# The order in which a selective scan's input is loaded: two rounds of six channels

## The chip, the cores and the metric

The kernel runs on one core of one Trainium2 chip. The metric is the device time of one execution in microseconds (us); the kernel before was run three times, and its median counts.

## What is computed

The reference is a network of four layers over four images of 64 x 64 pixels with 96 channels. Layers 0 and 1 are of one kind, and nearly all of the time lies in them. Each normalises its input, projects it to 192 channels, applies a 3 x 3 convolution and a SiLU, and then runs a selective scan along the 4096 pixels in four directions (by rows, by columns, and both backwards). Cut to what matters:

```python
delta = softplus(dts @ dt_w + bias)             # for image, direction k, channel e, pixel l
def step(h, inp):                               # 16 states n for every channel
    u, d, b, c = inp
    h = exp(d[..., None] * A) * h + d[..., None] * b[:, :, None, :] * u[..., None]
    y = einsum('bken,bkn->bke', h, c)
    return h, y
out = scan(step, h0, (u, delta, B, C)) + u * D
```

The four directions are added, normalised, gated by SiLU(z), projected back and added to the input. Layers 2 and 3 (linear attention and a quantised feed-forward block) follow, and the change does not touch them.

## The kernel before

**Stages.** `Scans.run` (L701) goes over four phases: two layers times two pairs of images. For each it runs `prepare` (normalisation, projection, convolution, delta and so on, interleaved with `finish` of the phase before) and then `scan_phase` (L471). At the end `token_layers` does layers 2 and 3.

**What `prepare` leaves in DRAM.** `steps` (L285) writes delta as three bf16 parts, B and C (`ph.bc`), and the product delta * u as float32 (`ph.du`, L160). The product is written twice: `ph.du` is laid out [2 copies, G = 8 rows, 192 channels + 2, 512 pixels], where a row is one image in one direction.

**The scan stage.** A unit is a chunk of 512 pixels and a block of 12 channels (EB), for all 8 rows and 16 states at once: 128 partitions are 8 rows times 16 states. There are 8 chunks x 16 blocks = 128 units in a phase. For one unit:

- `load` (L386) takes a buffer `h` of 128 partitions x 12 channels x 512 pixels (four buffers), loads delta by `load_delta` (L374, the tile `dlt`, 72 partitions) and delta * u by six calls of `load_quarters` (L396). Every row of `du` is broadcast to four partitions of a quarter. A quarter is 32 partitions; partitions 32 to 95 are filled by one DMA that reads both copies (768 KB), the upper quarter (96 to 127) by one that reads copy 1, the lower one (0 to 31) by one that reads copy 0 (384 KB each). All of these carry six channels (n = EB // 2), so there are two DMAs for each of the three groups of partitions.
- `times_b` (L408, the multiplication at L411) multiplies h by B on POOL, three channels at a time: four instructions a unit. It runs six channels (B_LEAD) ahead of the scans.
- `replicate` and `decay` (L413, L419) make exp(delta * A): a matmul of PE spreads delta over the partitions, and ACT takes the exponential.
- `scan` (L425, the instruction at L428) is one scan along the pixels on DVE for each channel: twelve a unit.
- `contract` (L437) multiplies by C and sums over the states on PE one unit later, `evict` copies the sum to SBUF, and `store` (L462) writes it with four DMAs to `ph.y`.

**What sets the order.** The scan stage lies within a manual schedule: every engine works through its instructions in the order in which the program issues them, written out by hand in L508 to L544. At the end of unit `at` SP's queue gets, in this order: the four stores of unit `at - 1`, sometimes a load of B or C, and the loads of unit `at + 3` (delta first, then the six of h). The buffer of unit `at + 3` is that of unit `at - 1`, whose contraction ends in unit `at`. Every DMA that SP issues signals one of eight semaphores in turn, and waits first for the DMA that used this semaphore before, eight DMAs earlier. A POOL product waits for the loads that wrote its three channels: the products of channels 0 to 5 for the three DMAs of the first six channels, the others for the other three.

The part of `load` that matters:

```python
n = EB // 2
for first, quarters in ((1, 2), (3, 1), (0, 1)):
    for e in range(0, EB, n):
        self.load_quarters(u, e, n, first, quarters)
```

`first` is the first quarter that is written and `quarters` how many: (1, 2) is partitions 32 to 95, (3, 1) the upper quarter, (0, 1) the lower one.

Of the kernel before, what the change touches and what calls it, by code (L numbers as in the profile page):

```python
# [32 lines left out]
EB = 12  # L33
# [49 lines left out]
class Consts:  # L83
# [3 lines left out]
    def load(self, pool, name, shape):  # L87
        t = pool.tile(shape, F32, name=name)
        self.nc.sync.dma_start(t, self.a[name])
        return t  # L90
# [40 lines left out]
class Scans:  # L131
# [19 lines left out]
    def prepare(self, ph):  # L151
# [16 lines left out]
        with self.tc.tile_pool(name="prep", bufs=1) as wp, self.tc.tile_pool(  # L168
# [3 lines left out]
            def load(name, shape, at=0):  # L172
                t = wp.tile([at + shape[0]] + shape[1:], F32, name=name)
                nc.sync.dma_start(t[at:], a[pre + name])
                return t

            xp = load("x_proj", [C, 2, 2, XD2])
            dt_w = load("dt_w", [XD2 - 2 * NS, 2, E], at=2 * NS)
            conv_b = load("conv_b", [C, 2])
            ds = load("Ds", [C, 2, K])  # L180
            dsum = wp.tile([C, 2], F32, name="dsum")
# [204 lines left out]
    def load(self, u):  # L386

        nc, ph = self.nc, u.ph
        u.h = self.units.tile([128, EB, TC], F32, name="h", bufs=4)
        self.load_delta(u)  # L390
        n = EB // 2
        for first, quarters in ((1, 2), (3, 1), (0, 1)):
            for e in range(0, EB, n):
                self.load_quarters(u, e, n, first, quarters)

    def load_quarters(self, u, e, n, first, quarters):  # L396
# [594 lines left out]
```

## Time and profile before

| | |
|---|---|
| median of three runs | 12278.37 us (12270.65 to 12295.46) |
| the profiled execution | 12285.39 us, of which the span 12283.6 us |
| the four scan stages | 743 to 2650, 3556 to 5458, 6366 to 8270 and 9176 to 11079 us of the span |
| busy in the first of them (1907 us) | DVE 1805 us, POOL 1755 us, PE 1444 us, ACT 1287 us; DMA engines 0.74 on average, 249 GB/s |
| loads of h (L401) | 1024 DMAs of 768 KB and 2048 of 384 KB |

The scan stages take 7616 us of the 12283.6 us. A profile describes one execution, and its durations come from this one alone. A row of the page's group table gives the line, the engine, the operation, what is written and read, the number of instructions, then their busy time and the mean of one in ns, and last the engine's idle time ahead of them with what ended most of it. In the waits a row gives who waited for whom, the sum in us, how often, and the longest wait. "DMA share" is the mean busy share of the core's 16 DMA engines. The chain of waits follows the work that ended last back to the start of the span.

### The profile page before, as it was taken

The page shows a single profiled execution, that of the slowest core. Times are in us where ns is not written, and L with a number is a line of the kernel's source. Part 1 is how long each engine was busy: PE and PEld are TensorE (multiplying, and loading weights), DVE is VectorE, ACT ScalarE, POOL GpSimd, SP SyncE. Part 2 cuts the span into 40 slices and gives each one's busy share as a digit, 9 for nine tenths or more (in the row PEclk, how much of TensorE's full clock was granted, in tenths as well). Part 3 has the DMA queues.
Part 4 walks back from the last instruction along what each step waited for, and adds up shares of the span by engine and source line. Part 5 has one row for each costly group of instructions (what it writes and reads, how often), then busy time and mean ns, then how long its engine had stood idle before and what let it go on. Part 6 is the DMA issues. An engine that isn't in the chain of part 4 may idle for free.

```text
span 12283.6 us, 340681 instructions
## 1 busy us (share of the span) xinstructions
PE 9393.5 (76%) x147008; PEld 4897.8 (40%) x147008; DVE 9369.7 (76%) x9235; ACT 7066.9 (58%) x11815; POOL 7389.7 (60%) x2316
## 2 busy tenths in 40 slices
PE   7757777769877777769877777778877777777777
PEld 2224444433334444433334444443334444444333
DVE  2479999963569999982569999993459999993667
ACT  2456666643456666653456666662446666662556
POOL 0159999950149999970129999980119999990000
PEclk8669898889778988889778988888778888988787
DMA  3577777754667777764667777764567777773110
GB/s 94 170 226 256 251 252 252 251 166 140 205 206 253 251 252 255 252 201 123 183 206 253 252 251 254 251 226 125 173 194 250 253 253 252 252 252 124 19 21 11
DMA packets 906195, 2491.48 MB, mean 203 GB/s; under 512 B 278030, under 2 KB 560756, under 8 KB 773236
## 3 DMA queue, kind: packets, MB, share of 16 engines
q1 hardware_dynamic: 578036, 2163.43, 52.6%
q10 hardware_dynamic: 326656, 306.25, 8.5%
q8 instruction: 1158, 18.97, 0.7%
q14 instruction: 345, 2.83, 0.1%
HBM read 1955.47 MB, written 513.80 MB: 201 GB/s over the span
## 4 chain that ended last, share of the span: by engine, by line
DMA 57%; PE 20%; SPq 9%; DVE 5%; ACT 4%; issue 3%; POOL 1%; ACTq 1%; DVEq 0%; POOLq 0%
DMA h<-du 51%; SPq L401 8%; PE c L263 8%; PE f L596 2%; PE d L309 2%; DMA yk<-y 2%; DMA delta<-parts 1%; PE c L292 1%; PE f L687 1%; PE f L605 1%; DMA du<-du_sb 1%; POOL parts L323 1%; PE f L676 1%; DVE parts L324 1%; PE f L662 1%
## 5 line engine op out<-in xcount | busy, mean ns | idle before, releaser
L411 POOL TENSOR_TENSOR h<-h,b 128x1536 f32<-128x1536 f32 x2048 | 7019.3, 3461 | 603.8 <-DMA h<-du 230.7
L428 DVE TENSOR_TENSOR_SCAN h<-a,carry,h 128x512 f32<-128x512 f32 x5376 | 6346.6, 1259 | 238.3 <-POOL h L411 231.9
L421 ACT ACTIVATE a<-a,a_col 128x512 f32<-128x512 f32 x6144 | 4030.4, 664 | 1917.7 <-PE a L417 1885.8
L446 PEld LDWEIGHTS y<-h,cw 128*32 128x32 f32 x131072 | 2789.8, 129 | 3520.4 <-issue 1302.1
L446 PE MATMUL y<-h,cw 128*32 128x48 f32 x131072 | 3663.3, 266 | 537.8 <-DVE h L428 210.6
L417 PE MATMUL a<-dlt,rep 72*128 72x512 bf16 x6144 | 2562.4, 428 | 1339.9 <-DVE h L428 1242.8
L323 POOL CAST parts<-dl 96x1024 bf16<-96x1024 f32 x256 | 342.1, 1351 | 3108.6 <-DVE dl L320 2742.6
L319 DVE TENSOR_TENSOR du_sb<-dl,xc 96x1024 f32<-96x1024 f32 x256 | 397.0, 1577 | 1294.6 <-ACT dl L317 1242.0
L458 ACT COPY d<-y 128x384 f32<-128x384 f32 x2048 | 979.7, 478 | 490.5 <-PE y L446 449.4
L263 PE MATMUL c<-xn,taps 96*96 96x512 f32 x2304 | 1036.8, 611 | 73.7 <-DVE xn L248 52.8
L428 DVE TENSOR_TENSOR_SCAN h<-a,h 128x512 f32<-128x512 f32 x768 | 873.0, 1203 | 176.9 <-ACT a L421 139.2
L417 PEld LDWEIGHTS <-rep 72*128 72x128 bf16 x6144 | 490.8, 99 | 888.7 <-issue 646.5
L309 PE MATMUL d<-xd,dt_w 7*96 7x512 f32 x1024 | 523.0, 859 | 260.0 <-ACT xd L295 227.4
L263 PEld LDWEIGHTS c<-xn,taps 96*96 96x96 f32 x2304 | 383.6, 168 | 709.9 <-issue 631.2
L828 POOL MEMSET tn<- 1x4096 f32 x8 | 28.0, 3533 | 863.2 <-PE pa L848 514.2
L270 ACT ACTIVATE xc<-c,conv_b 96x512 f32<-96x512 f32 x128 | 87.3, 682 | 716.0 <-PE c L263 646.4
L596 PE MATMUL f<-yk,perm 128*128 128x384 f32 x1024 | 417.3, 547 | 96.6 <-DMA yk<-y 87.2
L324 DVE TENSOR_TENSOR parts<-dl,parts 96x1024 bf16<-96x1024 f32 x256 | 366.9, 1455 | 154.3 <-POOL parts L323 154.3
L317 ACT ACTIVATE dl<-d 96x1024 f32<-96x1024 f32 x256 | 252.0, 1017 | 402.3 <-DMA delta<-parts 230.6
L292 PE MATMUL c<-xc,x_proj 96*103 96x512 f32 x512 | 422.1, 961 | 2.5 <-ACT xc L270 2.5
L309 PEld LDWEIGHTS d<-xd,dt_w 7*96 7x96 f32 x1024 | 152.3, 212 | 548.3 <-ACT xd L295 299.0
L363 ACT ACTIVATE cw<-c,gmask 128x256 f32<-128x256 f32 x512 | 285.7, 569 | 119.2 <-DMA c<-bc 61.9
(114 smaller groups left out, 5656.7 us busy)
## 6 DMA issues: line engine op xcount, KB each, us to landing
h<-du SPq DMA_DIRECT2D x1024, 768.0 KB
h<-du SPq DMA_DIRECT2D x2048, 384.0 KB
delta<-parts ACTq DMA_DIRECT2D x512, 288.0 KB
dlt<-delta SPq DMA_DIRECT2D x512, 288.0 KB
du<-du_sb SPq DMA_DIRECT2D x256, 384.0 KB
du<-du_sb ACTq DMA_DIRECT2D x256, 384.0 KB
y<-d SPq DMA_DIRECT2D x2048, 48.0 KB
yk<-y SPq DMA_DIRECT2D x256, 384.0 KB
```

The source lines that it names most:

```text
L263: nc.tensor.matmul(rows(ps[:C]), taps[:, tap, h * C : (h + 1) * C], xn[:, ROWS * c + dy : ROWS * (c + 1) + dy, dx : dx + HW], start=tap == ...
L292: nc.tensor.matmul(rows(ps[:XD2]), xp[:, k, h], u[:, h], start=h == 0, stop=h == 1)
L309: nc.tensor.matmul(ps[:, m], dt_w[part, k, m * C : (m + 1) * C], xd[part], start=True, stop=True)
L324: nc.vector.tensor_tensor(parts[:, 2], delta, parts[:, 1], ALU.subtract)
L401: self.nc.sync.dma_start(u.h[32 * first : 32 * (first + quarters), e : e + n].rearrange("p e t -> p (e t)"), source.rearrange("a g e t -> ...
L411: self.nc.gpsimd.tensor_tensor(h, h, b, ALU.mult)
L417: self.nc.tensor.matmul(u.a[n], self.cst.rep[:, h], u.dl[:, e], start=True, stop=True)
L421: self.nc.scalar.activation(u.a[n], u.a[n], AF.Exp, scale=u.ph.a_col[:, at : at + 1])
L428: self.nc.vector.tensor_tensor_scan(u.h[:, n], u.a.pop(n), u.h[:, n], 0.0 if u.c == 0 else u.ph.carry[:, at : at + 1], ALU.mult, ALU.add,)
L446: self.nc.tensor.matmul(view(u.y[32 * j : 32 * j + 32], l2 * EB, (8 * EB, 4), (1, EB)), u.ph.cw[u.c][:, l1, 8 * j + l2], view(u.h, 64 * l1 ...
L458: self.nc.scalar.copy(u.d[:, :, :, l1], u.y[:, : 32 * EB].rearrange("p (t h x) -> p t h x", t=4, h=2))
L596: nc.tensor.matmul(ps[:, : 4 * C].rearrange("p (w v e) -> p w v e", w=4, v=nv), cst.perm[:, k], view(t, off, (sw if k < 2 else -sw, 4), (1 ...
```

## The change

The two loops of `load` change places, so that all partitions get channels 0 to 5 before any gets channels 6 to 11, and the lower quarter comes before the upper one:

```diff
         n = EB // 2
-        for first, quarters in ((1, 2), (3, 1), (0, 1)):
-            for e in range(0, EB, n):
+        for e in range(0, EB, n):
+            for first, quarters in ((1, 2), (0, 1), (3, 1)):
                 self.load_quarters(u, e, n, first, quarters)
```

The number of DMAs, their sizes, their sources and what they write stay the same. On PE, ACT, DVE and POOL the instructions and their order are the same in both kernels; on SP only these six DMAs of a unit stand in another order.

## Prediction

> **What bounds the kernel now.** I read the page's engine shares and its chain first, then the waits of SP's queue, then the rate of the scans, and last the DMA queues in short windows. Names: a unit's six loads of h are M0 and M1 (partitions 32 to 95, channels 0 to 5 and 6 to 11), U0 and U1 (96 to 127), L0 and L1 (0 to 31); r0 to r3 are POOL's four products (L411) of three channels each. The page, its chain and two costly groups:
>
> ```profile
> DMA 57%; PE 20%; SPq 9%; DVE 5%; ACT 4%; issue 3%; POOL 1%; ACTq 1%; DVEq 0%; POOLq 0%
> ...
> L411 POOL TENSOR_TENSOR h<-h,b 128x1536 f32<-128x1536 f32 x2048 | 7019.3, 3461 | 603.8 <-DMA h<-du 230.7
> L428 DVE TENSOR_TENSOR_SCAN h<-a,carry,h 128x512 f32<-128x512 f32 x5376 | 6346.6, 1259 | 238.3 <-POOL h L411 231.9
> ```
>
> DMA leads the chain, though DVE is over 90% busy in the scan stages. DVE's idle time comes from POOL, and POOL's from DMA. Next the scans of 1600 us of the first scan stage, and an unbroken run of them:
>
> ```profile
> 1000.00:2600.00 1600.00, 1539.77 (x1306) 0.89 0.74 252
> ```
>
> ```profile
> 2002.68 33.19 DVE L428 TENSOR_TENSOR_SCAN h<-a,carry,h 128x512 f32<-128x512 f32 x28 [1.39 <-POOL h L411]
> ```
>
> 1600 / 1306 x 12 gives 14.70 us for a unit; unbroken, DVE needs 33.19 / 28 x 12 = 14.22 us, and POOL's four products 13.7. So 0.48 us of a unit is lost, always ahead of r0, which needs M0, U0 and L0. What holds the loads back is seen in SP's own waits in that window:
>
> ```profile
> SPq L401 <- DMA h<-du: 488.9, 303, 3.6
> ...
> SPq L401 <- POOL h L411: 6.2, 13, 0.7
> SPq L401 <- PE a L417: 5.4, 6, 1.0
> ```
>
> Each DMA of SP waits for the landing of the one eight before it, and this, not a buffer (POOL, PE), is what SP waits for. M0 is issued a median of 9 us after the unit whose end allows it. The queue is always full: the scan stages are bound by DMA at 14.7 us a unit.
>
> **The DMA engines.** Three windows of the first loads; columns are window, its length, PE, PEld, DVE, ACT, POOL, clock, DMA share, GB/s:
>
> ```profile
> 748.20:749.40 1.20, 1.20 (x5) 0.37 (x3) 0.00 (x0) 0.00 (x0) 0.00 (x0) 0.50 0.97 410
> 753.50:756.50 3.00, 0.00 (x0) 0.00 (x0) 0.00 (x0) 0.00 (x0) 0.00 (x0) 0.50 0.98 205
> 759.00:760.40 1.40, 0.00 (x0) 0.00 (x0) 0.00 (x0) 0.00 (x0) 0.00 (x0) 0.50 0.50 211
> ```
>
> From 759.0 only U1 or L loads run: half of the 16 engines, 211 GB/s. From 748.2 M0 and M1 run: all engines, 410 GB/s. From 753.5 all engines are busy too and move only 205 GB/s: by the order of issues, these are U packets of unit 0 on one half of the engines beside M0 and M1 of unit 1 on the other half. Their 12 KB packets last 930 to 950 ns instead of 460. The chain shows what that costs:
>
> ```profile
> 746.24 14.63 DMA h<-du
> 760.88 18.11 DMA h<-du
> 779.01 19.28 DMA h<-du
> 798.31 14.27 DMA h<-du
> ```
>
> The links of the next two loads are about 4 us longer than those around them.
>
> [...]In the trace the lower engines' order is that of the issues.
>
> So the lower eight engines carry all of U and L and half of M[...]; the upper eight carry M's other half[...]. [...]
>
> **The change, part by part.** It removes and adds no instruction: PE, ACT, DVE and POOL keep their order, and so do stores and delta loads. Bytes per engine are the same. Only the six loads of a unit change places: M0 M1 U0 U1 L0 L1 becomes M0 L0 U0 M1 L1 U1.
>
> *Base.* A lower engine moves four 12 KB packets of each load: 24 x 0.466 us (12,288 x 8 / 211 GB/s) = 11.2 us, plus 6 x 0.155 = 0.9 of delta and 0.5 of y: 12.6 us. Of the 14.7 us measured, 2.1 are contention. Following single engines' back-to-back packets, M0 takes some 2.4 us, M1 2.1, L1 2.3, U0 and L0 1.9.
>
> *Products released earlier.* r0 waits for the first three loads instead of the first, third and fifth, r2 for the last three. The last load still lands last. Behind a late r2 on POOL stand r3 and the next unit's r0; DVE's scan 6 waits for it. While DMA sets the pace this gains only at a stage's end, at most 14.2 - 7.1 - 1.9 = 5 us; the last three units of the first stage ran without a stall (36 scans on end), so I take 2.5 us x 4 = 10 us.
>
> *M1's upper half moves beside U0.* With M0's issue as zero, the median issues are 0, 2.65, 4.96, 5.69, 6.43 and 7.13 us, the first packet follows some 1.5 us later. The lower engines start M0 at 2.9, the second load at 5.6, the third at 8.0 (quartiles 1 us on either side). Now M1 is fourth: its upper half starts at 5.69 + 1.5 = 7.2 us. L0 (1.9 us, less than M1's 2.1) follows M0, so U0 runs from about 7.3 to 9.2: the same time. Both halve, as from 753.5. Fully aligned, an engine loses 4 x 0.466 = 1.86 us; with engines apart by about 1 us, I take 0.9 (bounds 0 and 1.86).
>
> *M0's upper half stands beside the U1 of the unit before.* [...]The upper half starts at 1.5 us; the lower engines end their sixth load at 0.9, 2.0 and 4.1 us (quartiles). What is left then is lost: 0, 0.5 and 1.86, about 0.7 (bounds 0.2 and 1.86).
>
> *What goes.* M1's upper half no longer runs beside delta and M0. Of the 0.6 and 0.3 us that M0 and M1 lose now, I take 0.4 back (bounds 0 and 0.5).
>
> *Sum.* 0.9 + 0.7 - 0.4 = 1.2 us a unit, for 4 x 128 = 512 units 614 us, less 10: about 600. Nothing hides it: the queue is the bound, and DVE and POOL only wait more. The profiled run took 12285.4 us (span 12283.6), 7 us over the median 12278.4; 12278 + 600 gives 12,880. The first loads of a stage may lose less than now; a few us, left out.
>
> **The rivals.** *Full collision*, 0.15: the loads slow, engines drift into step, and all eight U packets meet upper M packets, as in units 1 and 2: 3.7 - 0.4 = 3.3 us a unit, 1,690 us, 13,970 us; half of this rival lies below 13,600. For it: 18.11 and 19.28 us. Against it: the issues are spread over 7 us in the steady state. *No collision*, 0.06: [...]14.7 us stays, only the stage ends gain, up to 20 us: 12,258. *Faster*, 0.09: splitting M1 from delta and M0 saves 0.5 us, the collision costs almost nothing, the queue falls under DVE's 14.22 us; 0.48 x 512 + 20 = 266 us, 12,012. It decides where the collision costs under 0.4 us a unit, a ninth of the 3.7. For it: each first read of M is slow now (0.8 to 1.5 us). Against it: 205 GB/s where the two streams meet.
>
> **How the numbers follow.** My forecast, partial collision, has 0.70, and its own range goes from +0.4 to +2.6 us a unit, 12,480 to 13,600. No collision is within 0.2%, about what a measurement of this kernel can tell from no change. The range for 8 in 10 reaches down to 12,250, to take in no collision, and up to 13,600; about 0.17 is left out. Slower 0.85, same 0.06, faster 0.09.
>
> **What would show it.** Right: in 1000 to 2600 us fewer than 1,250 scans, a DMA share above 0.74 with fewer GB/s than 252, windows with all engines busy near 210 GB/s in the steady state, and POOL waiting ahead of r2, not r0. SP still waits for h loads. Wrong: 252 GB/s or more, or scans unbroken for several units[...].

## The result, and the profile after

The changed kernel takes 13,062.5 us in the median against 12,276.8: a ratio of 1.0636, 95% interval 1.0617 to 1.0654. That is 786 us more, or 1.53 us for each of the 512 units. The profiled execution has a span of 13,039.8 us. Its four scan stages take 8,398 us where they took 7,616: 782 us more, so the whole loss lies in them.

The page of the kernel after, its chain and the two groups shown before:

```profile
DMA 60%; PE 18%; SPq 9%; DVE 4%; ACT 4%; issue 3%; POOL 1%; ACTq 1%; DVEq 0%; POOLq 0%
...
L411 POOL TENSOR_TENSOR h<-h,b 128x1536 f32<-128x1536 f32 x2048 | 7027.5, 3454 | 1365.1 <-DMA h<-du 559.5
L428 DVE TENSOR_TENSOR_SCAN h<-a,carry,h 128x512 f32<-128x512 f32 x5376 | 6401.9, 1261 | 894.4 <-POOL h L411 860.0
```

The instructions last as long as before (3454 ns against 3461, 1261 against 1259), but POOL idles 1365 us ahead of its products instead of 604, and DVE 894 us instead of 238. The scans in the same 1600 us of the first stage (window, length, busy time of DVE with its number of scans, granted clock of TensorE, DMA share, GB/s):

```profile
1000.00:2600.00 1600.00, 1398.18 (x1176) 0.83 0.73 227
```

There are 1176 scans where there were 1306: 16.3 us a unit. The DMA engines are as busy as before (0.73 against 0.74) and move 227 GB/s instead of 252. SP's waits in that window (who waits for whom, us in all, times, longest):

```profile
SPq L401 <- DMA h<-du: 482.5, 270, 3.8
SPq L466 <- DMA h<-du: 159.9, 108, 3.0
...
SPq L401 <- PE a L417: 9.5, 11, 1.3
```

SP still waits for earlier loads and hardly for a buffer. Where the stall sits is seen in the runs of scans on DVE from 2000 us on (start, length, instruction, count, idle time ahead of it):

```profile
2017.16 7.16 DVE L428 TENSOR_TENSOR_SCAN h<-a,carry,h 128x512 f32<-128x512 f32 x6 [0.96 <-POOL h L411]
2025.55 7.16 DVE L428 TENSOR_TENSOR_SCAN h<-a,carry,h 128x512 f32<-128x512 f32 x6 [1.23 <-POOL h L411]
2034.07 7.16 DVE L428 TENSOR_TENSOR_SCAN h<-a,carry,h 128x512 f32<-128x512 f32 x6 [1.36 <-POOL h L411]
2041.49 7.16 DVE L428 TENSOR_TENSOR_SCAN h<-a,carry,h 128x512 f32<-128x512 f32 x6 [0.27 <-POOL h L411]
```

Here the scans come in groups of six, half a unit, with a stall ahead of each. Before, runs of 12 to 36 scans went through. The two stalls are not equal: over the 1600 us DVE idles 1.54 us a unit ahead of the first six scans and 0.52 us ahead of the last six, where before it was 0.55 us and nothing.

### The profile page after: what moved, and what is told of

Same layout as the page of the kernel before. It is cut to its first block, busy times and chain, and to the rows that moved or that the text cites. A ratio compares the mean times of both kernels' runs of the same rounds, so it can differ in the third digit from the quotient of the medians.

```text
span 13039.8 us, 340679 instructions
## 1 busy us (share of the span) xinstructions
PE 9611.5 (74%) x147008; PEld 4963.5 (38%) x147008; DVE 9422.9 (72%) x9235; ACT 7176.7 (55%) x11815; POOL 7397.9 (57%) x2316
## 4 chain that ended last, share of the span: by engine, by line
DMA 60%; PE 18%; SPq 9%; DVE 4%; ACT 4%; issue 3%; POOL 1%; ACTq 1%; DVEq 0%; POOLq 0%
DMA h<-du 55%; SPq L401 8%; PE c L263 8%; PE f L596 2%; PE d L309 2%; DMA yk<-y 1%; DMA delta<-parts 1%; PE c L292 1%; PE f L687 1%; POOL parts L323 1%; PE f L605 1%; PE f L676 1%; DVE parts L324 1%; DMA du<-du_sb 1%; PE f L662 1%
## 5 line engine op out<-in xcount | busy, mean ns | idle before, releaser
L411 POOL TENSOR_TENSOR h<-h,b 128x1536 f32<-128x1536 f32 x2048 | 7027.5, 3454 | 1365.1 <-DMA h<-du 559.5
L428 DVE TENSOR_TENSOR_SCAN h<-a,carry,h 128x512 f32<-128x512 f32 x5376 | 6401.9, 1261 | 894.4 <-POOL h L411 860.0
L417 PE MATMUL a<-dlt,rep 72*128 72x512 bf16 x6144 | 2743.4, 451 | 1866.7 <-DVE h L428 1786.8
L417 PEld LDWEIGHTS <-rep 72*128 72x128 bf16 x6144 | 528.2, 100 | 1243.9 <-issue 949.5
```

The lines of the kernel that those rows point to most:

```text
L411: self.nc.gpsimd.tensor_tensor(h, h, b, ALU.mult)
L417: self.nc.tensor.matmul(u.a[n], self.cst.rep[:, h], u.dl[:, e], start=True, stop=True)
L428: self.nc.vector.tensor_tensor_scan(u.h[:, n], u.a.pop(n), u.h[:, n], 0.0 if u.c == 0 else u.ph.carry[:, at : at + 1], ALU.mult, ALU.add,)
```

## The experiments

Twelve kernels were timed, each beside the kernel before. All but run 2, which exchanges the copies that are read, differ only in the order of a unit's loads, so I give each as that order. Ratios, with their 95% intervals, are to the kernel before, which took 12,284 to 12,295 us there. A diff is against the changed kernel unless the text says otherwise, and shows only the lines that matter. Three theories stood against each other. *Ports*, a name only, as no trace shows a port: a U load and the upper half of an M load slow each other where they meet, because of the partitions they write. *DRAM*: the two streams read the same copy of delta * u. *Split*: it costs to tear M0 and M1 apart. A fourth came up on the way, *queue*: the issue of the next unit's M0 waits for the fourth load, and comes too late where this is M1.

Lower and upper engines are names too, for two groups of eight that the trace tells apart by when the parts of a load land. In the kernel before, M0 of the first stage's second unit is issued at 749.31 us. Its semaphore is updated 16 times: eight times from 756.3 to 757.9 us, beside the U loads of the first unit, and eight times from 765.2 to 767.7, after these, L0 and L1, which land one after the other at 753.7 to 755.6 (U0), 757.5 to 759.3 (U1), 759.4 to 760.9 (L0) and 761.3 to 763.3 (L1). So eight engines, the lower ones, carry U, L and half of M in the order of issue; the upper ones carry the other half of M, its upper half. That this half is the one written to partitions 64 to 95 is the author's assumption: the trace gives no addresses.

**Run 1, both rounds with the upper quarter first** (M0 U0 L0 M1 U1 L1):

```diff
-            for first, quarters in ((1, 2), (0, 1), (3, 1)):
+            for first, quarters in ((1, 2), (3, 1), (0, 1)):
```

> The two rounds of six channels stay, but in both the upper quarter is loaded before the lower one: M0 U0 L0 M1 U1 L1. Ports theory (only a U load beside the upper half of M costs[...]): the upper half of M1 then runs beside L0, that of M0 beside L1 of the unit before, [...]so the whole loss goes: 14.2 to 14.7 us a unit, 12,020 to 12,280 us. Split theory (a round costs because M0 and M1 are torn apart and POOL waits twice a unit): as the changed kernel, about 13,060. DRAM theory (U and the upper half of M read the same copy of delta * u): as the ports theory, since U moves away from M.

Measured: 12,513.9 us, 1.0182 (1.0167 to 1.0197). Exchanging U and L in the rounds takes 549 of the 786 us away, so the rounds alone are not the cause. But 222 us stay, which none of the theories had forecast.

**Run 2, the copies exchanged** (the changed kernel's order, U reads copy 0 and L copy 1):

```diff
-        copies = slice(0, 2) if quarters == 2 else slice(first % 2, first % 2 + 1)
+        copies = slice(0, 2) if quarters == 2 else slice(1 - first % 2, 2 - first % 2)
```

> The changed kernel's order, but the lower quarter reads copy 1 and the upper quarter copy 0 (both copies hold the same numbers). Ports theory: what is written where doesn't change, so 13,060 within 60 us. DRAM theory (the loss comes from two streams that read the same copy): U then reads the copy that the upper half of M doesn't read, and the loss goes, about 12,280. Split theory: 13,060.

Measured: 13,037.9 us, 1.0599 (1.0579 to 1.0620). As slow as the changed kernel, within 0.4%. It doesn't matter which copy is read: the DRAM theory falls. What is left of the exchange in run 1 is where a load writes, and when.

**Run 3, lower quarter first in the first round only** (M0 L0 U0 M1 U1 L1):

```diff
-        for e in range(0, EB, n):
-            for first, quarters in ((1, 2), (0, 1), (3, 1)):
-                self.load_quarters(u, e, n, first, quarters)
+        for e, order in ((0, (0, 3)), (n, (3, 0))):
+            self.load_quarters(u, e, n, 1, 2)
+            for first in order:
+                self.load_quarters(u, e, n, first, 1)
```

> M0 L0 U0 M1 U1 L1: only the first round has the lower quarter first, so only the meeting of U0 with the upper half of M1 is left; beside the upper half of the next unit's M0 stands L1. Ports theory: 0.9 to 1.0 us a unit of the 1.55, 14.68 + 0.9 = 15.6 us, about 12,740 (12,550 to 12,900). Split theory: 13,060.

Measured: 12,725.1 us, 1.0354 (1.0338 to 1.0369): 0.85 us a unit over before, where I had 0.9 to 1.0. Run 7 will show that this is the sum of a larger loss and a gain.

**Run 4, lower quarter first in the second round only** (M0 U0 L0 M1 L1 U1), as run 3 with the two orders exchanged:

```diff
+        for e, order in ((0, (3, 0)), (n, (0, 3))):
```

> M0 U0 L0 M1 L1 U1: only the second round has the lower quarter first, so only the meeting of U1 with the upper half of the next unit's M0 is left. Ports theory: 0.6 to 0.7 us a unit, 15.3 us, about 12,600 (12,400 to 12,800); its loss and that of the run with the other meeting alone add up to the 786 us of the change. Split theory: 13,060.

Measured: 12,891.5 us, 1.0494 (1.0468 to 1.0519). This is above the range, and the losses of runs 3 and 4 over before, 434 and 600 us, add up to more than the change's 786. Taken from run 1 instead, 211 and 378 us are 589, against 549 from run 1 to the changed kernel. So the two meetings seem to come on top of something that run 1 has too. The window 1000 to 2600 us of run 3, then of run 4:

```profile
1000.00:2600.00 1600.00, 1455.65 (x1230) 0.87 0.76 237
```

```profile
1000.00:2600.00 1600.00, 1427.48 (x1199) 0.84 0.70 231
```

The two lose in different ways. Run 3 has busier DMA engines than before (0.76) that move less (237 GB/s): slow packets. Of the packets of 12 KB, 72 a unit last over 0.7 us there, in run 4 49 and before 35. Run 4 has engines that stand idle (0.70): the queue runs dry. Fewer than eight packets are in flight for 1.40 us of a unit, in run 3 for 0.18 us.

**Run 5, the quarters exchanged, the old nest kept** (M0 M1 L0 L1 U0 U1):

```diff
-        for e in range(0, EB, n):
-            for first, quarters in ((1, 2), (0, 1), (3, 1)):
+        for first, quarters in ((1, 2), (0, 1), (3, 1)):
+            for e in range(0, EB, n):
```

> The other part of the change alone: the loop nest of before, but the lower quarter ahead of the upper one: M0 M1 L0 L1 U0 U1. Ports theory: U1 (and the end of U0) stands beside the upper half of the next unit's M0, M1 beside M0: the price of that meeting in the fourth run, 12,514 to 12,892 us, so 0.74 us a unit, 12,290 + 380 = 12,670 (12,550 to 12,850). Split theory (only tearing M0 and M1 apart costs): as before, 12,290.

Measured: 12,175.5 us, 0.9910 (0.9895 to 0.9925). Both theories miss: this is faster than before, though U1 stands beside the next M0. The meeting is there in the trace: from 2 to 4 us after the issue of M0, 13 packets of 12 KB a unit last over 0.7 us, against 9 before. So a U load at the end of a unit need not cost time; what stands ahead of it matters (run 12).

**Run 6, M0 and M1 together, the quarters in rounds** (M0 M1 U0 L0 U1 L1), with one list in place of the two loops:

```diff
+        for first, e in ((1, 0), (1, n), (3, 0), (0, 0), (3, n), (0, n)):
+            self.load_quarters(u, e, n, first, 2 if first == 1 else 1)
```

> M0 M1 U0 L0 U1 L1: M0 and M1 stay together as before and L1 last, only the four quarter loads go in two rounds, so that the first two products wait for four loads, not five. Ports theory: no U beside an upper half of M: 12,290 less the later gain, 12,250 to 12,300. Split theory: M0 and M1 are not torn apart, so the same.

Measured: 12,143.9 us, 0.9883 (0.9868 to 0.9898), 0.28 us a unit under before and better than I expected. Against the order of before only U1 and L0 have changed places.

**Run 7, M1 third, U0 behind it** (M0 L0 M1 U0 U1 L1); the loop of run 6 with this list:

```diff
+        for first, e in ((1, 0), (0, 0), (1, n), (3, 0), (3, n), (0, n)):
```

> M0 L0 M1 U0 U1 L1: M0 and M1 are torn apart by L0 alone; the upper half of M1 runs beside the lower engines' M0 and L0, U0 and U1 come after it, and beside the next M0 stands L1. Ports theory (the 222 us of the first run are late engines whose U0 still meets the upper half of M1): no loss, 12,290 to 12,350. Split theory (those 222 us come from M0 and M1 being apart): 12,500.

Measured: 12,120.4 us, 0.9859 (0.9844 to 0.9874). M0 and M1 are apart, and it is 0.34 us a unit faster than before, more than either theory had forecast: the split theory falls. From run 3 it differs in one exchange, U0 behind M1 instead of ahead of it: 1.0354 to 0.9859 is 608 us, 1.19 us a unit.

**Run 8, the order of before with delta later** (M0 M1 U0 U1 delta L0 L1), shown against the kernel before:

```diff
-        self.load_delta(u)
         for first, quarters in ((1, 2), (3, 1), (0, 1)):
+            if first == 0:
+                self.load_delta(u)
             for e in range(0, EB, n):
```

> The order of before, with the load of delta between U1 and L0 instead of ahead of M0: M0 M1 U0 U1 delta L0 L1. Delta is written to partitions 0 to 71, [...]by twelve engines; ahead of M0 four of the upper engines write it beside L1. Ports theory: beside U those writes meet nobody, L1 and M0 lose less, 0.2 to 0.4 us a unit, and DVE's 14.22 us is the floor: 12,080 to 12,190. If delta's place doesn't matter: 12,290.

Measured: 12,019.2 us, 0.9781 (0.9765 to 0.9797), better than forecast: 265 us less than before. All waits of DVE's scans in 1000 to 2600 us:

```profile
DVE h L429 <- POOL h L412: 2.6, 7, 0.9
```

DVE waits 2.6 us in 1600: its own scans are now the bound. From 2 to 4 us after the issue of M0 under 2 packets of 12 KB a unit last over 0.7 us, where before 9 did, as the ports theory wants. But the 265 us are not the price of that alone. Delta also takes another place among the DMAs that wait for the one eight before, and M1 and U0 are issued 1.57 and 3.15 us after M0 instead of 2.70 and 4.97; no run keeps these two apart. The trace bears out the twelve engines of the expectation. In the kernel before, the semaphore of an M load is updated 16 times, that of a U or L load 9 times, once at a median of 1.1 us after the issue and eight times as it lands, and that of a delta load 13 times. The second unit's delta, issued at 748.45 us, has one update at 749.7, four from 753.9 to 754.6, before the lower engines were done with the first unit's loads, and eight from 763.1 to 765.5: four upper engines and the eight lower ones.

**Run 9, M1 fourth without a U ahead of it** (M0 L0 L1 M1 U0 U1); the loop of run 6 with this list:

```diff
+        for first, e in ((1, 0), (0, 0), (0, n), (1, n), (3, 0), (3, n)):
```

> M0 L0 L1 M1 U0 U1: M1 stands fourth, as in the changed kernel, but no U load is near its upper half: beside it stand L0, L1 and M1 itself, and U0 and U1 come last as in the fifth run, where they cost nothing. The issue of the next unit's M0 waits for the fourth load. Ports theory alone: as the fifth run, 0.2 us a unit under before, about 12,180. Queue theory (with M1 fourth the next M0 is issued late, and lower engines run dry): over before, 12,350 to 12,650, with a DMA share of 0.70 to 0.73 in the window where before has 0.74.

Measured: 12,290.9 us, 1.0002 (0.9993 to 1.0012), with a DMA share of 0.74. That is between the two: M1 in the fourth place costs 0.22 us a unit over run 5, which also ends in U0 U1, and the engines don't stand idle more. The queue theory explains a small part of the 786 us at most.

**Run 10, M1 third, U0 ahead of it** (M0 U0 M1 L0 U1 L1); the loop of run 6 with this list:

```diff
+        for first, e in ((1, 0), (3, 0), (1, n), (0, 0), (3, n), (0, n)):
```

> M0 U0 M1 L0 U1 L1: M1 stands third, where it cost nothing in the seventh run, but U0 is ahead of it, so its upper half runs beside U0. The fourth load is L0. Ports theory: the meeting alone, 0.5 to 0.9 us a unit over the seventh run, 12,380 to 12,590, with a higher DMA share and fewer GB/s than there. Queue theory alone: as the seventh run, about 12,125.

Measured: 12,710.8 us, 1.0338 (1.0312 to 1.0364). This is above the range. From run 7 it differs in that U0 and L0 have changed places; that costs 588 us, 1.15 us a unit. M1 is third in both, so its place in the queue is not the cause. Over 1000 to 2600 us the DMA share is the same as in run 7 (0.75), with 237 GB/s against 256; it is in short windows that the meeting stands out. Here are windows of 1 us, eight us after the issue of M0, in three units on end; columns are window, length, TensorE's clock, DMA share, GB/s. First run 7, where L0 and M1 itself stand beside the upper half of M1:

```profile
2010.40:2011.40 1.00, 1.00 0.86 336
2025.40:2026.40 1.00, 1.00 0.72 295
2038.80:2039.80 1.00, 1.00 0.82 338
```

Then run 10, where U0 stands beside it:

```profile
2014.60:2015.60 1.00, 1.00 0.94 233
2032.50:2033.50 1.00, 0.91 0.92 210
2047.00:2048.00 1.00, 0.50 0.92 209
```

More engine time is busy and a third less is moved. The same microsecond of all units of the 1600 us gives 333 GB/s on average in run 7 and 229 in run 10. Per unit, 33 packets of 12 KB last over 0.7 us in run 7 and 70 in run 10. 209 and 210 GB/s are what half of the engines moved alone in the first loads (211), and what all 16 moved there when U met M (205).

**Run 11, the orders of runs 7 and 8 together** (M0 L0 M1 U0 U1 delta L1); the list of run 7, with delta loaded ahead of L1 and no longer ahead of M0:

```diff
+            if (first, e) == (0, n):
+                self.load_delta(u)
```

> The orders of the seventh and eighth runs together: M0 L0 M1 U0 U1 delta L1. The eighth run has 14.1 us a unit, where DVE's scans alone set the pace, so only the ends of the stages can gain: 12,000 to 12,030 us. If delta so late, beside M0 of the next unit, takes from L1 what it gave: 12,100.

Measured: 11,987.6 us, 0.9747 (0.9732 to 0.9762). It is a little under the forecast and beats both kernels, the one before by 2.5%. DVE from 2000 us on:

```profile
1999.20 201.02 DVE L428 TENSOR_TENSOR_SCAN h<-a,carry,h 128x512 f32<-128x512 f32 x171
```

171 scans go through without a stall, 1.176 us each: 14.1 us a unit. While the scans take this long, no order of the loads can do better in the steady state.

**Run 12, run 7 with its last two loads exchanged** (M0 L0 M1 U0 L1 U1):

```diff
-        for first, e in ((1, 0), (0, 0), (1, n), (3, 0), (3, n), (0, n)):
+        for first, e in ((1, 0), (0, 0), (1, n), (3, 0), (0, n), (3, n)):
```

> M0 L0 M1 U0 L1 U1: the seventh run with its last two loads exchanged, so that U1 stands beside the upper half of the next unit's M0, while M1 is third and U0 behind it. If that meeting costs by itself what it cost in the fourth run against the first (378 us, 0.74 a unit): 12,500. If it costs only where the lower engines have been thrown apart already by a U0 ahead of M1: within 60 us of the seventh run, 12,070 to 12,190.

Measured: 12,411.7 us, 1.0109 (1.0086 to 1.0132). That is 307 us over run 7, 0.60 us a unit, between the two forecasts and nearer to the first. So L1 U1 at the end costs also where U0 is behind M1. Run 5 ends in U1 too and was cheap. The two orders differ in more than one place, but run 9 also ends in U0 U1 and is cheaper than run 12 too. That points to the fifth load: U0 in runs 5 and 9, L1 here.

## Why the prediction was right, step by step

**The bound.** Right. DMA set the pace before and after; SP waits for loads in both, and no engine has more work. Runs 8 and 11, where DVE goes through unbroken, show the other side: with fewer slow packets (28 and 30 a unit against 35 before), DVE's scans are the bound.

**The meetings.** That U and the upper half of M slow each other was right: eight us after M0, run 10 moves 229 GB/s where run 7, with L0 in U0's place, moves 333. Runs 2, 7 and 10 leave the place written as what matters, not the copy read and not the split: U0 and L0, which change places between runs 7 and 10, are alike in size (384 KB) and in the number of engines (nine updates each). Why the place matters was the author's assumption; no run shows it. In us a unit, from runs that differ in one exchange:

| exchange | runs | cost |
|---|---|---|
| U0 ahead of M1 instead of behind it, or instead of L0 | 7 to 3, 7 to 10 | 1.19, 1.15 |
| L1 U1 at the end instead of U1 L1 | 3 to after, 7 to 12, 1 to 4 | 0.68, 0.60, 0.74 |
| run 7 against before | before to 7 | -0.34 |

-0.34 + 1.19 + 0.68 is the 1.53 of the change by construction; the second numbers of each row, from other pairs, give 1.41.

*M1's upper half beside U0.* This is the term that was mis-sized: I took 0.9, it is 1.15 to 1.19. The 12 KB packets alone take 9.81 us a unit in runs 3 and 10, as a mean of the 16 engines, and 8.78 in run 7; these 1.03 us are most of it. I had spread the engines about 1 us apart and so let part of U0 pass before M1 came; less passes, it seems, than I took. In the changed kernel the meeting also comes later than I had it, because the fourth load is issued 6.59 us after M0 and not 5.69: most of the slow packets lie 8 to 11 us after M0. The exchange from run 7 to run 3 also puts M1 in the fourth place, for which run 9 against run 5 shows 0.22; from run 7 to run 10 it does not, and the cost is the same.

*M0's upper half beside U1.* I took 0.7; 0.60 to 0.74 were measured. The price is right, its reason only in part, so that its size is luck. Run 5 has the same meeting and is no slower than before. What fits all the orders is an assumption: two transfers arrive on the upper engines at the end of a unit, first the part of delta that four of them carry, which L slows as U slows M, then M0. With U1 L1 at the end (runs 6 and 7) both would then pass free, with L0 L1 (before) delta meets L, with U0 U1 (run 5) M0 meets U, with L1 U1 (the changed kernel, run 12) both meet. The traces show the two apart. A unit's second load waits for the landing of the fifth of the unit before, its third for the sixth, eight DMAs earlier each. Medians of 1000 to 2600 us; slow packets are those of 12 KB that last over 0.7 us, from 2 to 4 us after M0:

| last two loads | runs | second load after M0, us | third after second, us | slow packets a unit | fewer than eight packets in flight, us a unit |
|---|---|---|---|---|---|
| U1 L1 | 1, 3, 6, 7, 10 | 2.03 to 2.15 | 2.07 to 2.52 | 7.7 to 8.3 | 0.05 to 0.33 |
| L0 L1 | before | 2.70 | 2.32 | 8.9 | 0.15 |
| U0 U1 | 5, 9 | 1.98, 2.00 | 3.08, 3.18 | 13.1, 13.5 | 0.18, 0.36 |
| L1 U1 | changed kernel, 2, 4, 12 | 2.44 to 2.82 | 3.10 to 3.25 | 10.3 to 14.2 | 0.44 to 1.40 |

An L as the fifth load makes the second late by about half a microsecond, a U as the sixth makes the third late by some 0.6 us or more. Only where both come together does the queue run dry for long. So U1 beside M0 seems to cost most through the late third load, and only where the second is late already. That it is delta that slows the fifth load is argued from the orders and from the slow packets that go in run 8.

*What goes.* I took back 0.4, because M1's upper half would leave delta and M0. Run 7 is indeed 0.34 under before, but so is run 6 by 0.28, in which M1 is where it was. The gain came from the order at the end of the unit, U1 ahead of L1. The step had the right size by luck, for a wrong reason.

**The sum.** 1.2 us a unit against 1.53: 600 us forecast, 786 measured. The difference is mostly the first meeting, 1.19 instead of 0.9.

**Products released earlier.** I wrote that POOL would wait ahead of r2, not r0. It waits ahead of both, and longer ahead of r0: over 1000 to 2600 us it idles 1.87 us a unit ahead of r0 and 0.75 us ahead of r2. The stall ahead of r2 goes with rounds that end in L1 U1: it is 0.99 us in run 4 as well, but 0.08 us in run 3, whose rounds have the other meeting alone. No gain from the earlier release is seen in the steady state. At the ends of the stages it fits what I took: from the issue of a stage's last load to its last scan the changed kernel needs 23.9 to 24.2 us, the one before 27.4 to 28.2, which makes 15 us for the four against my 10. Part of this may be the last load itself, which is U1 instead of L1.

**What would show it.** The scans (1176, under 1,250) and the GB/s (227, under 252) were as forecast; the DMA share was not: 0.73, where I wanted more than 0.74. Slow packets raise it (0.76 in run 3), but engines that run dry lower it (0.70 in run 4). With U1 slowed, it lands late; the third load, eight DMAs on, waits for it, and all issues behind it are late too. After M0's issue the third follows at a median of 5.87 us in the changed kernel and at 4.65 in run 7. Between 7 and 8 us after that issue the changed kernel's engines are busy 0.51 of the time on average, run 7's 0.97. A share of half is what the lower engines alone make (0.50 from 759.0 in the first loads), since M1 is fourth here; that even these run dry is seen in the 0.76 us of a unit with fewer than eight packets in flight, against 0.13 in run 7. I had counted slow packets alone. The windows near 210 GB/s are there in run 10. In the changed kernel the engines are busy 0.97 of the time from 9 to 11 us after M0 and move 251 GB/s on average: slow, but not all packets at once.

**The rivals.** *No collision* did not come in the changed kernel. Runs 6 and 7 show what an order without these meetings takes, and it is less than I had: 12,144 and 12,120 us, not 12,258. *Faster* named the floor rightly, DVE's scans, but it takes another order to get there (runs 8 and 11). *Full collision* didn't come: 3.3 us a unit against 1.53.

**Open.** Run 1 loses 0.43 us a unit, 0.78 over run 7, though no U stands directly ahead of an M. M1 in the fourth place explains 0.22 of it, from run 9. The rest is probably late engines whose U0 still meets the upper half of M1, two places on. The trace supports it: from 7 to 10 us after M0, 23 packets of 12 KB a unit last over 0.7 us in run 1, 40 in run 3 where U0 stands directly ahead of M1, 9 in run 9 and 2 in run 7. It doesn't tell which load a packet belongs to, and no run tests it.

## What to carry to other kernels

Before changing the order of transfers, find out for each which engines carry it and which partitions it writes, and then which two will be in flight at the same time; a window with all engines busy and half the GB/s is the sign of a meeting (0.98 and 205 GB/s here, where M loads alone had 0.97 and 410). To release a consumer earlier brought nothing that could be seen here while the transfers set the pace. Where each DMA waits for the landing of one a fixed number of places before, one slow transfer delays the issue of those behind it (here the third load follows M0 after 5.87 us instead of 4.65), and two slow ones in a row can leave the engines without work (fewer than eight packets in flight for 0.44 to 1.40 us of a unit in the orders that end in L1 U1). Try the places of small transfers too: moving one of 288 KB was worth 265 us here.

## What the runs showed of the hardware that was not expected

A U load and the upper half of an M load, on 16 engines together, moved 205 GB/s in the first loads and 229 on average eight us after M0 in run 10, hardly more than U1 or L loads on eight engines (211). In the same place of run 7, L0 and M1 itself beside the upper half of M1 moved 333 on average, and M loads alone 410 in the first loads. Which of two copies in DRAM the slowed stream reads makes no difference (13,038 against 13,062 us).

The order of the same transfers alone moved this kernel from 11,988 to 13,062 us, 9%, with the same bytes and the same instructions.
